# Half-size weight pieces, the extremes of the second weight taken inside the loop, and two row sums of each convolution's last half made from VectorE's moments

## The chip, the cores and the metric

The kernel runs on one core of a Trainium2 chip. Its engines are TensorE (PE, with its weight loads PEld), VectorE (DVE), ScalarE (ACT), GpSimd (POOL) and SyncE (SP), each with its own queue of instructions in a fixed order; transfers between HBM and SBUF run on 16 DMA engines and are issued here from SP and, a few, from ScalarE. The metric is the time of one execution on the device in microseconds: the median of three runs before the change is 2258.8 us (2254.0 to 2258.85).

## The reference

Two layers on an image batch x of shape (8, 256, 56, 56) in float32, each added to its input:

```python
x = x + involution(group_norm(x))      # layer 0
x = x + tri_block(group_norm(x))       # layer 1

def involution(x):                      # 7x7 kernels made per pixel, 16 groups
    ker = w_span @ (w_reduce @ x + b_reduce) + b_span
    out = (ker * patches_7x7(x)).sum(axis=3)

def tri_block(x):
    out1 = relu(batch_norm(noised_tri_conv(x, w1)))
    out2 = batch_norm(noised_tri_conv(out1, w2))
    return relu(out1 + out2)

def noised_tri_conv(x, w):              # 3x3, 256 to 256 channels
    tw = w - mean(w)
    mx, mn = max(tw), min(tw)
    lo, hi = mn + (mx - mn) / 3, mx - (mx - mn) / 3
    tq = where(tw < lo, -1, where(tw > hi, 1, 0))
    return conv(x, tq) + einsum(x, tq[:, :, 1, 1])
```

Two things matter for the change. A weight can be made ternary only when its mean, maximum and minimum over all its elements are known. And batch_norm needs the mean and variance of a convolution's whole output, over all eight images, before anything behind it can begin.

## The kernel before

The kernel has four stages, one after the other.

**The start** (L591 to L922). SP loads the first image (L545), then both weights whole into one buffer, `wf` (L631, four transfers), then 16 stores of zeros from the tile `xn` into the DRAM scratch `xtd` (L637). GpSimd may fill `xn` with data only when these stores have read it. `params(0)` finds group norm's factors of image 0. A loop over the three rows py of a tile then runs, for each, one strip of `prep` (GpSimd's `spread` into xn, a transpose on TensorE, ScalarE's copy into `stg`, a store to xtd), `reduce` (the pk matrix products, L651, copied into `kr` by ScalarE, L656), and three steps of `found`. `found` chains the searches for the extremes of both weights (`extremes`): for each sixth of a weight (768 elements in each partition) VectorE takes a maximum (L208) and a minimum (L209), and ScalarE a sum (L210, in place). When the sixths are done, two small steps on TensorE combine the partitions (`ends_w`, L222; `all_w`, L230), and some ten tiny VectorE instructions make mean, lo and hi in `cols`. After that `generate(0, 0, ...)` makes the first quarter's matrices: 14 units of pg matrix products (L782), each read out of PSUM into `a` by VectorE (L791) and ScalarE (L786). The pg products have two PSUM buffers. Further strips, the tile xe's parts (`surround`) and steps of `found` are put between the units.

**The loop** (L940 to L988) has 32 quarters of images with ten rows each, 320 rows. A row applies the matrices (pa, L815, on TensorE), picks the result out (L827 on ScalarE, L828 on VectorE, L831 on GpSimd), and, for the next quarter and the next image, does one or two units of `generate`, a strip, a part of xe, statistics (L150) and loads. `pin` keeps the order of the text on every engine. From row 8 on, every row also takes one step of `quant`, which makes the weights ternary and transforms them for the convolution: 16 pieces of each of the two weights, seven steps a piece, with one piece buffer (`piece_of`). A piece is fetched (L257), compared with hi and lo (L261, L262), subtracted (L264), combined into planes (L277 to L284) and stored (L287) by way of the list `tasks`, which `transfer` empties at the head of a row. In `params`, one step apart, TensorE makes `br` (L576) from the new factors and VectorE adds it into `brn` (L579).

**Two convolutions** (`conv_phase`) run over 16 half images each. For each, six groups of products (L464, in ORDER 1, 2, 3, 4, 0, 5) are combined into four interleaved rows y. Their sums and sums of squares are taken by ScalarE with an accumulating activation (`sums`, L416), one half image behind. In the last half image there is no half image left behind which to do that: `last_rows` takes rows 1 and 2 after group 4, row 0 after group 0, and row 3 after group 5, each of the latter two with four activations of 392 elements and a read of the accumulator for each. `batch_norm_params` (L177 and on) adds the columns of `stats` up; the columns are 2B + 2, since the last half image has three.

**The final stage** (L1052 to L1065) reads y1, y2 and x1 back tile by tile (16 tiles of 1.6 MB of each), combines them with two activations and two VectorE instructions, and stores the output. y1 and y2 have two buffers, x1 three. The first activation of a tile needs only the first convolution's factors; everything else needs the second's.

Of the kernel before, what the change touches and what calls it, by code (L numbers as in the profile page):

```python
# [80 lines left out]

QN, QJ = 96, 3 * C // 96
QS = WT
SLOT = (0, 2, 3, 4, 5, 1)
QM = 6


@with_exitstack
def involution_tri_block_kernel(
# [20 lines left out]
    def const_tile(shape, name):  # L110
        return const.tile(shape, F32, tag=name, name=name)
# [11 lines left out]

    st1, st2 = (const_tile([P, CT, 2, 2 * B + 2], name) for name in ("st1", "st2"))

# [66 lines left out]
    def piece_of(pool, name):  # L192
        return pool.tile([P, (4 + QS) * QN], F32, tag="piece", name=f"piece_{name}")

    def extremes(w, cols, pool, transposer, psum_tile, name):

# [6 lines left out]

        s, mx, mn = col(QM), col(QM), col(QM)
        f = nf // QM
        for j in range(QM):
            v = w[:, j * f:(j + 1) * f]
            nc.vector.tensor_reduce(mx[:, j:j + 1], v, AX.X, ALU.max)  # L208
            nc.vector.tensor_reduce(mn[:, j:j + 1], v, AX.X, ALU.min)  # L209
            nc.scalar.activation(v, v, AF.Identity, accum_out=s[:, j:j + 1])  # L210
            yield
        sums, ends = col(), col(2)
# [5 lines left out]
        nc.vector.memset(v[:, :P], 1.0)  # L218
        yield

        ps = psum_tile(f"ends_{name}")
        nc.tensor.matmul(ps[:, P:P + 1], v[:, :P], sums, start=True, stop=True)  # L222
        nc.tensor.transpose(ps[:2, :P], ends, transposer)
        mean, top = cols[:, 0:1], col()
        nc.vector.tensor_scalar(mean, ps[:, P:P + 1], 1.0 / (P * nf), None, ALU.mult)
        nc.vector.tensor_reduce(top[:2], ps[:2, :P], AX.X, ALU.max)
        nc.vector.tensor_copy(v[:2, P:2 * P], top[:2].to_broadcast([2, P]))
        yield
        ps = psum_tile(f"all_{name}")
        nc.tensor.transpose(ps[:, :2], v[:2, P:2 * P], transposer[:2, :2])  # L230
        ex = col(2)
        nc.vector.tensor_copy(ex, ps[:, :2])
# [4 lines left out]

        d, q0, r, th = (col() for _ in range(4))
        nc.vector.tensor_tensor(d, amx, amn, ALU.subtract)
# [7 lines left out]

    def quantize(dst, w_dram, cols, pool, tasks, name):


        mean, lo, hi = (cols[:, k:k + 1] for k in range(3))
        for t in range(CT):
            for j in range(QJ):
                v = piece_of(pool, name)
                w, u = v[:, :3 * QN], v[:, 3 * QN:]
                o = (t * QJ + j) * 3 * QN
                nc.sync.dma_start(w, w_dram[:, o:o + 3 * QN])  # L257
                yield
                yield
                g = u[:, :3 * QN]  # L260
                nc.vector.tensor_scalar(g, w, mean, hi, ALU.subtract, ALU.is_gt)  # L261
                nc.vector.tensor_scalar(w, w, mean, lo, ALU.subtract, ALU.is_lt)  # L262
                yield
                nc.vector.tensor_tensor(g, g, w, ALU.subtract)  # L264

                def part(x, k):
                    return x[:, k * QN:(k + 1) * QN]


                c0, c1 = max(C, j * QN) - j * QN, min(2 * C, (j + 1) * QN) - j * QN  # L270
                if c0 < c1:
                    g1 = part(u, 0)[:, c0:c1]
                    nc.vector.tensor_scalar(g1, g1, 2.0, None, ALU.mult)

                e, f = part(w, 0), part(w, 1)
                g1, g0, g2 = (part(u, k) for k in range(3))
                nc.vector.tensor_tensor(e, g0, g2, ALU.add)  # L277
                yield
                nc.vector.scalar_tensor_tensor(f, g2, 4.0, g0, ALU.mult, ALU.add)
                nc.vector.tensor_tensor(part(u, 3), e, g1, ALU.add)  # L280
                nc.vector.tensor_tensor(part(u, 4), e, g1, ALU.subtract)
                yield
                nc.vector.scalar_tensor_tensor(part(u, 5), g1, 2.0, f, ALU.mult, ALU.add)
                nc.vector.scalar_tensor_tensor(part(u, 6), g1, -2.0, f, ALU.mult, ALU.add)  # L284

                def store(u=u[:, QN:], o=t * 3 * C + j * QN):
                    nc.sync.dma_start(  # L287
                        bass.AP(dst[:].tensor, dst[:].offset + o,
                                [[QS * CT * 3 * C, P], [CT * 3 * C, QS], [1, QN]]), u)

                tasks.append(store)
                yield
                yield

# [20 lines left out]
    def conv_phase(i, begun, src_d, norm, stats, shift, dst_d, follow):  # L315
# [104 lines left out]
        def last_rows(n, y, k0, m):  # L420

            for _ in sums(n, [y[:, to].rearrange("p (r k) -> p r k", k=4 * W)
                              [:, :, k0 * W:(k0 + m) * W] for to in range(CT)]):
                pass

        done = iter(())
        nxt, begun = {}, ({}, None)
# [6 lines left out]
        for n in range(2 * B):  # L434
# [22 lines left out]
            for k in ORDER:  # L457
# [34 lines left out]
                elif k == 0:  # L492
                    row_of(0, m[0], 1.5, s, ALU.add)
                    if final:
                        last_rows(n + 1, y, 0, 1)
                elif k == 5:
                    row_of(3, m[5], 6.0, d, ALU.add)
                    if final:
                        last_rows(n + 2, y, 3, 1)
                next(steps, None)  # L500
# [17 lines left out]
    with ExitStack() as ph1:  # L518
# [6 lines left out]
        def ps_one(name):  # L525
            return ps_a.tile([P, 512], F32, tag="pt", name=name)
# [30 lines left out]
        def params(b):  # L557
# [13 lines left out]
            prm[b], prm_edge[b] = dst, edge  # L571
            yield
            ps = ps_one(f"br_{b}")
            for c in range(NCQ):
# [48 lines left out]
        for v in xe:  # L623
            nc.gpsimd.memset(v, 0.0)

        nf = CT * 9 * C
        wf = apool1.tile([P, A_COLS], F32, tag="a1", name="wf")
        for i, v in enumerate((w1, w2)):
            for j in range(2):
                o = j * nf // 2  # L630
                nc.sync.dma_start(wf[:, i * nf + o:i * nf + o + nf // 2], v[:, o:o + nf // 2])  # L631
        zero = xn.rearrange("p k r x -> p (k r x)")

        for d in (d for ds in xt_d for d in ds):
            for r0, n in ((0, PAD), (PAD + HH, HQ - PAD - HH)):
                e = n * QX * RP // P
                nc.sync.dma_start(  # L637
                    bass.AP(d[:].tensor, d[:].offset + r0 * QX * RP, [[e, P], [1, e]]), zero[:, :e])

        def reduce(b, py):  # L640
# [251 lines left out]
        for _ in params(0):  # L892
            pass
        strips, around = prep(0), surround(0, 0)
        a_next = matrices(0)
        thresholds = [pieces.tile([P, 32], F32, tag=f"cols{i}", name=f"cols{i}") for i in range(2)]
        ext = [extremes(wf[:, i * nf:(i + 1) * nf], thresholds[i], pieces, ident_sb, ps_one, f"w{i}")
               for i in range(2)]

        found = chain(*(islice(v, QM) for v in ext), *ext)  # L900

        for py in range(PY):
            next(strips)
            transfer(len(tasks))
            reduce(0, py)
            for _ in range(3):
                next(found)
# [25 lines left out]
        for k in rows[:QLEAD]:  # L933
            transpose_q(*k)
        pin()
        norm = iter(())
        quant = chain(*(quantize(wq_d[i], v, thresholds[i], pieces, tasks, f"w{i + 1}")
                        for i, v in enumerate((w1, w2))))
        last = None
# [197 lines left out]
```

## Time and profile before

| what | value |
|---|---|
| median of the runs | 2258.8 us |
| the profiled execution, whole | 2269.48 us |
| its span, first to last instruction | 2267.7 us |
| mean granted TensorE clock | 0.924 |
| PE busy | 1866.4 us, 82% |
| DVE busy | 1706.7 us, 75% |
| ACT busy | 1268.3 us, 56% |
| POOL busy | 584.5 us, 26% |
| HBM traffic | 264.05 MB read, 142.48 MB written |

In the trace the first row of the loop begins at 79.4 us, the last of its rows ends near 1149, the first convolution's products run from 1155.95 to 1584.7, the second's from 1600.7 to 2029, and the final stage from there to the end. A row of the loop takes some 3.4 us. The page's second part divides the span into 40 equal slices, with a digit for each engine's busy tenths; a window gives the same for any stretch, in microseconds, with the DMA rate; the timeline lists instructions in order of time with the idle time before each and what ended it. An average over the whole span mixes stages with different limits, so each stage is read by itself.

### The profile page before, as it was taken

To read this page: it belongs to the slowest core of one execution; us is meant where nothing else is said; L and a number is where in the kernel's file an instruction comes from. 1 tells how busy PE (TensorE), PEld (TensorE's weight loads), DVE (VectorE), ACT (ScalarE), POOL (GpSimd) and SP (SyncE) were. 2 spreads that over 40 slices of the span, in tenths; PEclk is the share of its full clock that TensorE was granted. 3 is DMA by queue.
4 is the path that set the end of the run, shared out by engine and by line. 5 is a ranking of instruction groups with operands and counts; after the bars stand their busy time and mean duration, and the time that the engine had idled before them with its cause. 6 is when DMAs were issued, how large, how long until landed. Compare 5 with 4: busy or idle time off the path is not lost.

```text
span 2267.7 us, 72706 instructions
## 1 busy us (share of the span) xinstructions
PE 1866.4 (82%) x31088; PEld 1716.6 (76%) x31088; DVE 1706.7 (75%) x2906; ACT 1268.3 (56%) x2461; POOL 584.5 (26%) x1320
## 2 busy tenths in 40 slices
PE   4889899898998989999879999999799999970000
PEld 3778777777877877778779999999799999970000
DVE  6676857667585775655689999998999999975444
ACT  3555455455554645556446766665576666673434
POOL 2545546364563645546400000000000000000000
PEclk9899999999999999999989999999899999995555
DMA  6556646566474754645453333334333333369999
GB/s 211 154 157 181 199 131 206 147 192 189 131 221 120 225 164 138 197 119 160 138 206 116 129 134 140 119 116 161 133 138 117 116 116 116 116 255 401 410 430 403
DMA packets 156447, 411.24 MB, mean 181 GB/s; under 512 B 51550, under 2 KB 62172, under 8 KB 148444
## 3 DMA queue, kind: packets, MB, share of 16 engines
q1 hardware_dynamic: 150528, 376.56, 49.9%
q10 hardware_dynamic: 5596, 30.03, 3.2%
q8 instruction: 245, 4.01, 0.8%
q14 instruction: 78, 0.64, 0.1%
HBM read 264.05 MB, written 142.48 MB: 179 GB/s over the span
## 4 chain that ended last, share of the span: by engine, by line
PE 38%; DMA 7%; DVE 3%; ACT 1%; issue 1%; ACTq 0%; SPq 0%; POOL 0%; DVEq 0%
PE c L464 37%; DMA y1f<-y1d 3%; DMA x1f<-x1d 2%; DMA out_y<-x1f 1%; DVE x1f L1064 1%; DMA y2f<-y2d 1%; ACT dummy L416 1%; DVE y1f L1062 0%; ACT y1f L1061 0%; ACT y1f L1063 0%; PE pa L815 0%; PE ptq L749 0%; DVE q L346 0%; DVE r L366 0%; DVE u L373 0%
## 5 line engine op out<-in xcount | busy, mean ns | idle before, releaser
L464 PE MATMUL c<-pl,wq 128*128 128x392 f32 x4608 | 857.1, 348 | 20.2 <-ACT pl L351 20.2
L464 PEld LDWEIGHTS c<-pl,wq 128*128 128x128 f32 x4608 | 855.1, 189 | 22.0 <-ACT pl L351 20.7
L791 DVE TENSOR_TENSOR a<-pg,bt 126x756 f32<-126x756 f32 (+3 forms) x640 | 393.2, 656 | 192.7 <-ACT a L786 147.3
L782 PE MATMUL pg<-kr,wl 64*126 64x140 f32 (+1 forms) x6144 | 459.4, 294 | 14.3 <-DVE a L791 7.1
L782 PEld LDWEIGHTS pg<-kr,wl 64*126 64x126 f32 x6144 | 396.8, 196 | 66.4 <-issue 41.5
L815 PE MATMUL pa<-a,q 126*32 126x48 f32 x17920 | 273.2, 208 | 62.3 <-issue 38.5
L815 PEld LDWEIGHTS pa<-a,q 126*32 126x32 f32 x17920 | 223.1, 111 | 115.8 <-issue 53.4
L786 ACT ACTIVATE a<-pg,bt 126x126 f32<-126x126 f32 x768 | 243.3, 475 | 102.6 <-PE pg L782 102.4
L831 POOL TENSOR_TENSOR x<-x,inv 128x168 f32<-128x168 f32 x320 | 166.4, 520 | 438.5 <-DVE inv L828 375.5
L828 DVE SCALAR_TENSOR_TENSOR inv<-pa,half_sb,inv 128x168 f32<-128x168 f32 x320 | 117.1, 366 | 171.0 <-ACT inv L827 144.8
L351 ACT CAST pl<-r 128x812 fp32r<-128x812 f32 x192 | 162.5, 868 | 145.2 <-DVE r L346 126.9
L752 ACT COPY q<-ptq 126x384 f32<-126x384 f32 x320 | 138.2, 481 | 162.7 <-issue 96.2
L331 POOL MEMSET xp<- 128x116 f32 x32 | 6.3, 195 | 829.4 <-DVE a L346 829.4
L416 ACT ACTIVATE dummy<-y,nc 128x1568 f32<-128x1568 f32 (+2 forms) x144 | 210.1, 1459 | 5.3 <-DVE y L484 3.5
L674 POOL TENSOR_SCALAR xn<-x,gn 128x224 f32<-128x224 f32 (+2 forms) x384 | 179.1, 486 | 130.0 <-PE pt L717 70.8
L352 DVE TENSOR_TENSOR pl<-r,pl 128x812 fp32r<-128x812 f32 x192 | 187.2, 1002 | 28.2 <-ACT pl L351 27.0
L674 POOL TENSOR_SCALAR xe<-x,gn 128x168 f32<-128x168 f32 (+2 forms) x384 | 161.2, 439 | 0.0
L720 ACT COPY stg<-pt 98x512 f32<-98x512 f32 x128 | 74.9, 585 | 137.0 <-issue 88.5
L749 PE MATMUL ptq<-ident_sb,xe 128*126 128x128 f32 x960 | 144.2, 285 | 4.6 <-DVE var_a L170 2.6
L150 DVE BATCH_NORM_STATS2 st<-x 128x6 f32<-128x392 f32 x256 | 138.3, 557 | 11.8 <-DMA x<-in_x 10.2
L827 ACT ACTIVATE inv<-pa,half_sb 128x168 f32<-128x168 f32 x320 | 128.2, 401 | 26.8 <-PE pa L815 25.7
L1011 ACT ACTIVATE xp<-raw,gn 128x392 f32<-128x392 f32 (+1 forms) x124 | 82.6, 721 | 62.9 <-DVE a L346 58.9
(144 smaller groups left out, 1846.2 us busy)
## 6 DMA issues: line engine op xcount, KB each, us to landing
q<-xtd SPq DMA_DIRECT2D x320, 252.0 KB
raw<-x1d SPq DMA_DIRECT2D x32, 812.0 KB
raw<-y1d SPq DMA_DIRECT2D x32, 812.0 KB
x<-in_x SPq DMA_DIRECT2D x64, 392.0 KB
xtd<-stg SPq DMA_DIRECT2D x128, 196.0 KB
x1d<-x SPq DMA_DIRECT2D x64, 392.0 KB
y1d<-y SPq DMA_DIRECT2D x30, 784.0 KB
y2d<-y SPq DMA_DIRECT2D x30, 784.0 KB
```

Of the source, the lines that this page charges most:

```text
L150: nc.vector.bn_stats(st[:, j, :], xt[:, j * NC:(j + 1) * NC])
L351: nc.scalar.copy(hi, r)
L352: nc.vector.tensor_tensor(lo, r, hi.bitcast(F32), ALU.subtract)
L416: nc.scalar.activation(dst, v, f, bias=shift[:, to:to + 1], accum_out=stats[:, to, j, n:n + 1])
L464: nc.tensor.matmul(ps[:, to, :NM], wq[k][:, t, dx, to * P:(to + 1) * P], part[:, t, :, dx:dx + W], start=(c == 0), stop=(c == last))
L674: nc.gpsimd.tensor_scalar(dst[:, i - d - k0:f - d - k0, :, x0:x0 + n], v[:, i:f, :, j0:j0 + n], scale, bias, ALU.mult, ALU.add)
L749: nc.tensor.transpose(pt[:NQ, k * P:(k + 1) * P], xe[c % 2][:, k, PY * ty:PY * ty + QY].rearrange("p r x -> p (r x)"), ident_sb)
L782: nc.tensor.matmul(dst, wl[rows, c, gp, o:o + NQ], kr[py][rows, px, :], start=True, stop=True)
L786: nc.scalar.activation(whole[:, g0 + i, p0 + j], ps[:NQ, i, j * nt:(j + 1) * nt], AF.Identity, bias=bt[:, c, g0 + i, p0 + j:p0 + j + 1])
L791: nc.vector.tensor_tensor(dst[:, g0:g0 + 2, p0:p0 + nv].rearrange("q g p t -> q g t p"), ps[:NQ, :, t0 * nv:t1 * nv].rearrange("q i (t p) ...
L815: nc.tensor.matmul(ps[o:o + 32, k * 2 * n:(k + 1) * 2 * n], q[:NQ, k, o:o + 32], av[:, t + k, g * 2 * n:(g + 1) * 2 * n], start=True, stop ...
L831: nc.gpsimd.tensor_tensor(xv, xv, iv.rearrange("p t (y x) -> p y t x", x=PX), ALU.add)
```

## The change

- The 16 stores of zeros are issued ahead of the weight; only w1 is loaded at the start and searched there as before, in six sixths, with two steps of `found` in each pass of the py loop instead of three.
- w2 is searched inside the loop, between the quantizing of w1 and that of w2. It is fetched in 12 pieces of 384 elements, and VectorE takes the sum as well as the extremes.
- Pieces are half as long (48 output channels instead of 96), there are 32 of each weight, and the piece tile has two buffers. `paced` runs fetch, `ternary`, `planes_of` and `store` of a piece at fixed rounds (0, 2, 3, 6), two pieces in seven rounds. A store is issued in its own round, not by way of `tasks`. The weights' layout in DRAM follows the new sizes.
- In the last half image of a convolution, rows 0 and 3 are no longer summed by ScalarE: VectorE takes their moments (`row_stats`) and, after row 3, turns the moments of both into sums (`row_sums`). `stats` has one column less.
- `params` has one more yield before the br products.

The order in which the final stage's instructions are issued moves too, though its text does not: before, tiles 3 and 4, and 5 and 6, run in pairs on ScalarE, VectorE and SP and the tiles from the seventh on one by one; now they run one by one from the third tile on, and the third x1 load is issued behind the third y2 and y1 loads instead of ahead of them.

```diff
-QN, QJ = 96, 3 * C // 96
+QN, QJ = 48, 3 * C // 48
-QM = 6
+QM, QM2 = 6, 12
...
-        return pool.tile([P, (4 + QS) * QN], F32, tag="piece", name=f"piece_{name}")
+        return pool.tile([P, (4 + QS) * QN], F32, tag="piece", bufs=2, name=f"piece_{name}")
+    def paced(events):
+        for r in range(max(events) + 1):
+            for f in events.get(r, ()):
+                f()
+            yield
...
+        def fetch(j):
+            held[j] = piece_of(pool, name)[:, :f]
+            nc.sync.dma_start(held[j], w_dram[:, j * f:(j + 1) * f])
+        def seek(j):
+            v = w[:, j * f:(j + 1) * f] if w is not None else held[j]
             nc.vector.tensor_reduce(mx[:, j:j + 1], v, AX.X, ALU.max)
             nc.vector.tensor_reduce(mn[:, j:j + 1], v, AX.X, ALU.min)
-            nc.scalar.activation(v, v, AF.Identity, accum_out=s[:, j:j + 1])
-            yield
+            if w is not None:
+                nc.scalar.activation(v, v, AF.Identity, accum_out=s[:, j:j + 1])
+        def add(j):
+            nc.vector.tensor_reduce(s[:, j:j + 1], held.pop(j), AX.X, ALU.add)
+        events = {}
+        for j in range(n):
+            if w is not None:
+                events[j] = [lambda j=j: seek(j)]
+            else:
+                r = 5 * (j // 2) + j % 2 * 2
+                events.setdefault(r, []).append(lambda j=j: fetch(j))
+                events.setdefault(r + 2, []).append(lambda j=j: seek(j))
+                events.setdefault(r + 3, []).append(lambda j=j: add(j))
+        yield from paced(events)
...
+        events = {}
+        for k in range(CT * QJ):
+            r = 7 * (k // 2) + k % 2 * 3
+            for n, f in ((0, fetch), (2, ternary), (3, planes_of), (6, store)):
+                events.setdefault(r + n, []).append(lambda f=f, k=k: f(k))
+        yield from paced(events)
...
+        def row_stats(st, y, k, j):
+            for to in range(CT):
+                v = y[:, to].rearrange("p (r k) -> p r k", k=4 * W)[:, :, k * W:(k + 1) * W]
+                nc.vector.bn_stats(st[:, to, j], v)
+        def row_sums(n, st):
+            mv = st[:, :, 2, :2]
+            for to in range(CT):
+                nc.vector.bn_aggr(mv[:, to, :], st[:, to, :2].rearrange("p n s -> p (n s)"))
+            sq = st[:, :, 2, 2]
+            nc.vector.tensor_tensor(mv[:, :, 0], mv[:, :, 0], shift, ALU.add)
+            nc.vector.tensor_tensor(sq, mv[:, :, 0], mv[:, :, 0], ALU.mult)
+            nc.vector.tensor_tensor(mv[:, :, 1], mv[:, :, 1], sq, ALU.add)
+            nc.vector.tensor_scalar(stats[:, :, :, n], mv, 2.0 * HT * W, None, ALU.mult)
...
                     if final:
-                        last_rows(n + 1, y, 0, 1)
+                        moments = half("s2").rearrange("p o r w -> p o (r w)")[
+                            :, :, :18].rearrange("p o (n s) -> p o n s", s=6)
+                        row_stats(moments, y, 0, 0)
...
                     if final:
-                        last_rows(n + 2, y, 3, 1)
+                        row_stats(moments, y, 3, 1)
+                        row_sums(n + 1, moments)
...
-        for i, v in enumerate((w1, w2)):
-            for j in range(2):
-                o = j * nf // 2
-                nc.sync.dma_start(wf[:, i * nf + o:i * nf + o + nf // 2], v[:, o:o + nf // 2])
...
+        for j in range(2):
+            o = j * nf // 2
+            nc.sync.dma_start(wf[:, o:o + nf // 2], w1[:, o:o + nf // 2])
...
-        found = chain(*(islice(v, QM) for v in ext), *ext)
+        found = ext[0]
...
-            for _ in range(3):
+            for _ in range(2):
                 next(found)
...
-        quant = chain(*(quantize(wq_d[i], v, thresholds[i], pieces, tasks, f"w{i + 1}")
-                        for i, v in enumerate((w1, w2))))
+        made = [quantize(wq_d[i], v, thresholds[i], pieces, f"w{i + 1}")
+                for i, v in enumerate((w1, w2))]
+        quant = chain(made[0], ext[1], made[1])
```

## The prediction

> **What bounds the kernel now.** I read four views in this order: the page's slices, to split the span; the timeline of the start; windows by image for the long loop; timeline and windows of the two convolution ends and of the final stage. In the slices, PE and DMA busy tenths:
>
> ```profile
>
> DMA  6556646566474754645453333334333333369999
> ```
>
> A slice is 56.7 us. Slices 3 to 35 are TensorE's: the loop (320 rows, from 79 us to 1149) and two convolutions (1156 to 1584, 1601 to 2029). The first slice is not, and in the last four DMA is full. A removed stall at the start, or at a convolution's end, shortens the time at once; work added to VectorE in the loop counts only as far as TensorE waits for it; in the final stage only DMA gaps count. The start, from the timeline:
>
> ```profile
> 35.59 1.34 POOL L674 TENSOR_SCALAR xn<-x,gn 128x224 f32<-128x224 f32 x3 [31.85 <-DMA xtd<-xn]
> 36.98 1.09 PE L717 MATMUL pt<-ident_sb,xn 128*98 128x128 f32 x4 [5.59 <-POOL xn L674]
> ...
> 47.27 0.98 PE L782 MATMUL pg<-kr,wl 64*126 64x140 f32 x12
> ...
> 79.37 0.27 PE L815 MATMUL pa<-a,q 126*32 126x48 f32 x2
> ```
>
> Columns: start, duration, engine, instruction, and in brackets the idle time before it and what ended it. GpSimd may not overwrite xn until its zeros are in DRAM (L637), which SP issued behind both weights (L631); TensorE waits 5.59 us for it. 47.27 is the first matrix product of the first quarter, 79.37 the first row of the loop.
>
> **Start: two edits, one answer.** The zeros go ahead of the weight, and w2's 2.36 MB are not loaded here. DMA ran full from 10 to 30 us (349 to 424 GB/s in windows of 5 us). Images, constants and zeros are about 6.2 MB; by 25 us 7.7 MB had moved. So the zeros land near 25 us, not 35.5, and w1 (2.36 MB, 6 us at 400 GB/s) by about 30. VectorE's six pairs of reductions (12 x 0.86 us, start to start) then end near 37 to 39, ScalarE's sums following. TensorE ends its first pk group at 31.4 as before, transposes at once, and runs the two other groups (4.95 and 3.67 us) to about 40.5: first pg near 41, **6 us earlier**. ScalarE executes w1's sums in the same queue, ahead of the kr copies; should the weight land 4 us later, 4 of the 6 us are lost.
> From first pg to first pa took 32.1 us. Strips paced the first five units at 2.2 us; later TensorE idled 3.3 us before ends_w at 59.8 and 1.5 us before w2's at 67.7, and its clock fell to 0.52 to 0.79 in four windows of 5 us from 55 to 75. In the changed order six ScalarE sums of 1.03 us, five pairs of reductions (9 us of VectorE) and w2's ends_w and all_w leave this stretch. The strips' pace and ScalarE's 24 activations of a remain. Without the two stalls (4.8 us), and with a little less time at low clock, I estimate 26 us: another 6 us. **Start: -12 us, from -5 to -15.**
>
> **Loop: what is added.** Views by image (windows between every 40th L828):
>
> ```profile
> 353.00:491.00 138.00, 123.03 (x3314) 104.82 (x3312) 96.67 (x237) 73.74 (x201) 72.62 (x160) 0.99 0.58 169
> 629.00:766.00 137.00, 124.30 (x3316) 106.05 (x3314) 94.89 (x229) 73.41 (x202) 71.88 (x160) 0.98 0.62 174
> 905.00:1040.00 135.00, 124.15 (x3308) 106.37 (x3307) 81.95 (x179) 72.77 (x201) 69.95 (x160) 0.96 0.55 157
> ```
>
> Columns: window, length, busy us (count) of PE, PEld, DVE, ACT, POOL, clock, DMA share, GB/s. The third image has no quantizing (32 pieces x 7 rows from row 8 end at row 232). It has 13.8 us less VectorE than the mean of the two others and is about 2.5 us shorter: 0.18 us of time for 1 us of VectorE. VectorE's rows:
>
> ```profile
> L264 DVE TENSOR_TENSOR piece_w<-piece_w 128x288 f32<-128x288 f32 x32 | 15.8, 494 | 0.0
> L280 DVE TENSOR_TENSOR piece_w<-piece_w 128x96 f32<-128x96 f32 x32 | 8.8, 274 | 0.0
> ```
>
> Undisturbed they are 0.45 and 0.25 us, so about 0.15 us plus 1 ns an element. A piece is 3 of the first kind, 6 of the second and sometimes one of L273: 2.9 us. A half piece is 3 x 0.30 + 6 x 0.20 + 0.1 = 2.2; a pair 4.4: +1.5 us x 32 = 48 us. w2's extremes: 12 x 3 reductions of 384 elements, 0.55 each by the same line (the 768-element row took 0.95): 20 us. Together 68 us of VectorE, x 0.18 = **+12 us**.
> [...] But in the timeline independent 96-element instructions start 0.16 to 0.17 us apart though each lasts 0.25, so about 0.07 to 0.1 us of the fixed part is covered by the neighbour: 304 x 0.1 = 30 us, with w2's 17 us 47 us of occupied VectorE, x 0.18 = 8.5 us. Bounds: +3 (a fit over rows by quantizing phase gives a third of a us per 7 rows, 0.11 a us of VectorE, of 30 us) and +20 (0.3 a us). I take **+8**: the second sum, since the timeline shows the overlap.
> Hidden at no cost: SP's 64 fetches and 64 stores instead of 32 and 32, and w2's 12 fetches; SP waited over 410 us for pa in the loop, and the stores, now three rows behind their data, no longer hold it (104 us at L287). DMA share is 0.6: the 384-byte store packets took 24 ns each; 49,152 of 192 bytes at some 15 ns are 11 us more over 16 engines in 900 us. If that cover were gone, q loads would be late, and TensorE shows no such wait now. [...] Quantizing now ends at row 275, 45 rows before the loop does. The extra yield in params leaves br's matmuls at the same place on TensorE (seven waits of 1.6 us stay) and puts brn on VectorE behind two additions: nothing.
>
> **Convolution ends.**
>
> ```profile
> 1584.75 1.04 DVE L450 SCALAR_TENSOR_TENSOR y<-c,d 128x392 f32<-128x392 f32 x2 [1.44 <-PE c L464]
> ...
> 1590.29 0.23 DVE L177 TENSOR_REDUCE bmv_bn<-st 128x4 f32<-128x72 f32 x1 [4.50 <-ACT dummy L416]
> ...
> 2037.35 0.23 DVE L177 TENSOR_REDUCE bmv_bn<-st 128x4 f32<-128x72 f32 x1 [7.25 <-ACT dummy L416]
> ```
>
> L177 waits for ScalarE's row sums (0.75 us each, eight of 392 elements). They go. VectorE gets two bn_stats after row 0 (in its gap before row 3) and after row 3: 2 x 0.5, two aggregations (0.27, smaller here: 0.2), four tiny dependent steps (0.2 start to start): 2.3 us after 1585.75, so 1588.1. ScalarE's remaining sums end at 1584.3. Next late is VectorE itself. **-2.2 us**, and TensorE's second convolution starts so much earlier. At the second end row 3 is written at 2030.0, the sums are ready at 2032.3 (ScalarE's last at 2031.4): 5 us sooner. But DMA is full there:
>
> ```profile
> 2080.00:2090.00 10.00, 0.00 (x0) 0.00 (x0) 3.22 (x1) 0.00 (x0) 0.00 (x0) 0.50 0.92 341
> ...
> 2100.00:2110.00 10.00, 0.00 (x0) 0.00 (x0) 8.14 (x3) 6.39 (x3) 0.00 (x0) 0.50 0.96 375
> 2110.00:2120.00 10.00, 0.00 (x0) 0.00 (x0) 2.02 (x1) 0.69 (x1) 0.00 (x0) 0.50 0.91 385
> ...
> 2150.00:2160.00 10.00, 0.00 (x0) 0.00 (x0) 6.06 (x2) 2.91 (x1) 0.00 (x0) 0.50 1.00 428
> ```
>
> What counts is bytes not moved. Against 430 GB/s these three windows lack 1.9 MB, 4.4 us, and 2044 to 2056 lacks 0.7 MB, 1.7 us. The dips lie where the instructions run in pairs of images; the changed order leaves the pairing after the first pair, as the old order did from 2130 on at 428 GB/s. But one x1 load less is issued ahead of the wait at 2038, so a first dip stays. **-4 us, from -1 to -6.**
>
> **Sum:** -12 + 8 - 2 - 4 = -10 us: from the profiled execution's 2269.5 (span 2267.7) to 2259.5. The runs' median, 2258.8, lies 10.7 below the profiled one; the same -10 there gives **2249**.
>
> **Rivals.** (a) Forecast, 2244 to 2252: 0.48. (b) VectorE's work hides almost wholly (VectorE idles 300 us in the loop waiting for ScalarE): loop +3, others as said, -15: below 2244, centre 2242 with the start's upper bound: 0.22. For it: fit by rows; against it: the shorter third image. (c) The loop takes back nearly all: start only -8, loop +12, ends -4, the lower bounds but for the loop: no change, about 2259: 0.22. For it: ScalarE's sums of w1 stand ahead of the kr copies, and the clock may fall in the shorter start as well; against it: DMA was full there, so w1's landing follows from bytes alone. (d) Slower: longer VectorE blocks (1.2 us behind a row's additions, where 0.85 was the longest) push the additions that free pg's two PSUM buffers, TensorE waits at L782/L815. It decides from 0.37 us per us of VectorE (68 x 0.37 = 25 us against 18 gained, the rest being what a measurement can tell; at 0.45 the time is 2271): 0.08. For it: 23 existing pa waits for DVE a; against: those are 18.8 us in all.
> About 0.3%, 6.8 us, is what a measurement can tell from no change. So faster 0.70, same 0.23, slower 0.07. Range 2237 to 2263: it leaves out part of (d) and the end of (b).
>
> **What would show it.** First xn on POOL near 25 us, first pg near 41, first pa near 67; images 139 to 140 us up to row 275; L177 near 2.3 us after the last L450; final stage without windows under 400 GB/s after the first 20 us. The forecast is wrong if w1's late landing stalls the kr copies, if images are over 143 us, or if the final stage keeps its length.

## The result and the profile after

The changed kernel takes 2251.4 us (median of 20 runs, 2242.9 to 2261.4) where the kernel before takes 2258.6 beside it (20 runs, 2248.4 to 2269.8): ratio 0.9964, 95% interval 0.9951 to 0.9977, that is -8 us with -5 to -11. Beside later experiments the same kernel came to 0.9929 (0.9907 to 0.9951). In the three sets of the experiments the kernel before has medians of 2263.8, 2263.2 and 2262.1 us, and 2262.4 over all its 125 runs; the changed kernel's 26 runs have 2251.3. Over all sets the change is so worth -11 us (-10 to -13, by drawing the runs again at random). Medians of one kernel in different sets can differ by 5 us, and kernels that ran in different sets are to be compared with that in mind. The profiled execution of after took 2249.66 us (span 2247.9), 1.8 below its median; that of before stood 10.9 above the median of these 20 runs. So the 19.8 us between the two traces are not the effect, and each stage has to be read with that in mind.

The slices of the page of after, busy tenths of TensorE and of the DMA engines:

```profile
PE   5989898898989889889889999999899999980000
DMA  6647658475475755755453333334333333369999
```

TensorE's row in the page of before:

```profile
PE   4889899898998989999879999999799999970000
```

The structure is the old one: the first slice has a tenth more of TensorE, and no other stretch changes its character. By stage, from the starts of the first and last instruction of each in the two traces (us):

| stage | before | after | difference | predicted |
|---|---|---|---|---|
| start to first pg | 47.3 | 39.2 | -8.0 | -6 |
| first pg to first pa | 32.1 | 22.3 | -9.8 | -6 |
| loop, first pa to last picked row, as traced | 1068.0 | 1070.9 | +2.9 | |
| loop, set to the median | 1057.2 | 1072.6 | +15.4 | +8 |
| last product to first of the next convolution | 16.35 | 13.94 | -2.4 | -2.2 |
| the two convolutions together | 856.4 | 857.4 | +1 | 0 |
| last product to the end | 239.0 | 235.6 | -3.4 | -4 |

"Set to the median" takes from the loop what the profiled execution lies above the median of its kernel's runs. Three kernels of this study have the loop of before unaltered: before, e1_ends_only and e2_zeros_first. Their traced loops are 1068.0, 1057.7 and 1079.6 us, and their profiled executions lie 10.9, 0.1 and 20.3 us above their medians. The difference comes to 1057.2, 1057.6 and 1059.3. So the scatter of 20 us is in the loop, and the loop of before at the median is 1058; by the median of all 125 runs it is 1061. The loop's loss is 12 to 15 us.

**The start.** Timeline of after (start, duration, engine, instruction, idle time before it and what ended it):

```profile
25.78 1.34 POOL L734 TENSOR_SCALAR xn<-x,gn 128x224 f32<-128x224 f32 x3 [22.03 <-DVE brn L640]
29.35 0.95 DVE L223 TENSOR_REDUCE cols<-wf 128x1 f32<-128x768 f32 x1 [3.93 <-DMA wf<-in_w]
39.26 0.88 PE L842 MATMUL pg<-kr,wl 64*126 64x140 f32 x12
61.54 0.27 PE L875 MATMUL pa<-a,q 126*32 126x48 f32 x2
```

GpSimd no longer waits for its zeros: what releases it is the image's own brn. The weight is in at 29.3. Three windows of before in the stretch between first pg and first pa (window, length, busy us and count of PE, PEld, DVE, ACT, POOL, then granted clock, DMA share, GB/s):

```profile
57.00:62.00 5.00, 2.17 (x17) 1.95 (x18) 2.53 (x10) 2.50 (x9) 2.43 (x6) 0.57 0.43 120
62.00:67.00 5.00, 4.23 (x39) 3.46 (x37) 2.81 (x12) 2.44 (x7) 1.51 (x4) 0.75 0.57 184
67.00:72.00 5.00, 4.26 (x27) 3.46 (x28) 3.83 (x18) 0.00 (x0) 3.28 (x9) 0.59 0.09 30
```

and two of after in the same stretch:

```profile
49.00:54.00 5.00, 4.02 (x56) 3.32 (x52) 3.40 (x5) 2.69 (x8) 4.16 (x11) 1.00 0.89 275
54.00:59.00 5.00, 3.71 (x52) 3.02 (x50) 3.00 (x8) 2.34 (x7) 5.00 (x13) 1.00 0.37 104
```

Read the clock and the counts in parentheses together: TensorE is about as busy as in the second and third window of before, but with 52 to 56 matrix products in 5 us where it had 17 to 39. The two waits for ends_w are gone, and so is the low clock around them.

**The ends.** VectorE's timeline of after at the end of the first convolution, and the same step of the second:

```profile
1569.75 1.04 DVE L507 SCALAR_TENSOR_TENSOR y<-c,d 128x392 f32<-128x392 f32 x2 [0.49 <-PE c L521]
1570.70 1.03 DVE L470 BATCH_NORM_STATS2 s<-y 128x6 f32<-128x392 f32 x2
1571.64 0.33 DVE L476 BATCH_NORM_AGGREGATE s<-s 128x2 f32<-128x12 f32 x2
...
1572.88 0.22 DVE L177 TENSOR_REDUCE bmv_bn<-st 128x4 f32<-128x68 f32 x1
...
2015.80 0.22 DVE L177 TENSOR_REDUCE bmv_bn<-st 128x4 f32<-128x68 f32 x1
```

No idle time stands before L177: it follows 3.1 us after the start of the last row, where it was 5.5. Windows of the final stage of after:

```profile
2025.00:2030.00 5.00, 0.00 (x0) 0.00 (x0) 5.00 (x3) 2.91 (x1) 0.00 (x0) 0.50 0.86 316
...
2080.00:2090.00 10.00, 0.00 (x0) 0.00 (x0) 3.52 (x2) 5.40 (x2) 0.00 (x0) 0.50 1.00 428
2100.00:2110.00 10.00, 0.00 (x0) 0.00 (x0) 5.91 (x2) 2.91 (x1) 0.00 (x0) 0.50 1.00 424
2110.00:2120.00 10.00, 0.00 (x0) 0.00 (x0) 3.84 (x2) 4.67 (x2) 0.00 (x0) 0.50 1.02 435
```

The early dip stays, the later three are gone.

### The profile page after: what moved, and what is told of

Its sections match the earlier page's. It is cut to its first block, busy times and chain, and to the rows that moved or that the text cites. A ratio compares the mean times of both kernels' runs of the same rounds, so it can differ in the third digit from the quotient of the medians.

```text
span 2247.9 us, 73156 instructions
## 1 busy us (share of the span) xinstructions
PE 1849.4 (82%) x31088; PEld 1701.1 (76%) x31088; DVE 1757.2 (78%) x3246; ACT 1252.6 (56%) x2417; POOL 580.1 (26%) x1320
## 5 line engine op out<-in xcount | busy, mean ns | idle before, releaser
L521 PE MATMUL c<-pl,wq 128*128 128x392 f32 x4608 | 858.1, 349 | 17.8 <-ACT pl L391 17.8
L521 PEld LDWEIGHTS c<-pl,wq 128*128 128x128 f32 x4608 | 856.1, 190 | 19.6 <-ACT pl L391 18.3
L842 PE MATMUL pg<-kr,wl 64*126 64x140 f32 (+1 forms) x6144 | 447.6, 288 | 24.5 <-DVE a L851 14.2
L842 PEld LDWEIGHTS pg<-kr,wl 64*126 64x126 f32 x6144 | 385.2, 190 | 75.7 <-issue 42.8
L392 DVE TENSOR_TENSOR pl<-r,pl 128x812 fp32r<-128x812 f32 x192 | 187.1, 1001 | 29.3 <-ACT pl L391 28.1
L456 ACT ACTIVATE dummy<-y,nc 128x1568 f32<-128x1568 f32 (+1 forms) x128 | 200.1, 1563 | 4.8 <-DVE y L541 3.5
```

Source lines behind the costliest of these rows:

```text
L392: nc.vector.tensor_tensor(lo, r, hi.bitcast(F32), ALU.subtract)
L456: nc.scalar.activation(dst, v, f, bias=shift[:, to:to + 1], accum_out=stats[:, to, j, n:n + 1])
L521: nc.tensor.matmul(ps[:, to, :NM], wq[k][:, t, dx, to * P:(to + 1) * P], part[:, t, :, dx:dx + W], start=(c == 0), stop=(c == last))
L842: nc.tensor.matmul(dst, wl[rows, c, gp, o:o + NQ], kr[py][rows, px, :], start=True, stop=True)
```

## Experiments

The theory after the result: the start gave 18 us and the ends 6, and the loop took 12 to 15 of them back. The rivals: the loop is nearly untouched, and the gains of start and ends are smaller than one trace says; or a price that is not VectorE's, of SyncE's waits or of short packets, is what the loop pays. In the excerpts of code "..." stands for lines left out. All times are medians; ratios are to the kernel before on the same chip.

**1. The ends alone.** In before, with the two helpers and the narrower `stats` of the change:

```diff
-last_rows(n + 1, y, 0, 1)
...
+row_stats(moments, y, 0, 0)
...
-last_rows(n + 2, y, 3, 1)
+row_stats(moments, y, 3, 1)
+row_sums(n + 1, moments)
```

> The kernel before, with only the two row sums of the last half image moved to VectorE's moments. Theory A (both ends gain as the two traces show, -2.4 us between the convolutions and -3.4 us in the final stage): -6 us, 0.9974 of before; the statistics step L177 comes about 2.5 us after the last product of each convolution. Rival B (the final stage is bound by bytes, so its shorter length belongs to another order of its instructions or to chance, not to this edit): -2.4 us, 0.9989, and the stretch from the last product to the end stays at 239 us.

Measured: 0.9957 (0.9941 to 0.9973). The gap between the convolutions is 13.93 us, the last product stands 235.3 us before the end, as in the changed kernel. Theory A: 2.4 and 3.7 us. The final stage's gain comes with this edit, not with the rest of the change; whether by the earlier factors or by the other order of its instructions was not told apart. The ratio's middle, -10 us, is more than the trace's stages show; -6 is at the edge of its interval.

**2. The zeros first, alone.** In before, the block that loads wf, both weights, moves behind the stores of zeros:

```diff
-for i, v in enumerate((w1, w2)):
-    for j in range(2):
-        o = j * nf // 2
-        nc.sync.dma_start(wf[:, i * nf + o:i * nf + o + nf // 2], v[:, o:o + nf // 2])
 zero = xn.rearrange("p k r x -> p (k r x)")
 for d in (d for ds in xt_d for d in ds):
...
+for i, v in enumerate((w1, w2)):
+    for j in range(2):
+        o = j * nf // 2
+        nc.sync.dma_start(wf[:, i * nf + o:i * nf + o + nf // 2], v[:, o:o + nf // 2])
```

> The kernel before, with only the order of the start's transfers changed: zeros ahead of both weights, both weights still loaded and searched there. Theory A (the wait for xn was one of two causes): GpSimd's first xn at 25 us, first pg near 41, first pa near 72, -6 us or 0.9973 of before; the rest of the start's gain belongs to w2's search leaving it. Rival B (the start has slack behind the wait: the later landing of the weights takes the gain back at the extremes): first pa within 2 us of before's 79, ratio 1.000. Rival C (the order of the zeros is the whole gain of the start): first pa near 62, -16 us, 0.993.

Measured: 0.9983 (0.9961 to 1.0005); first pg 42.1, first pa 76.1. From TensorE's timeline of this kernel:

```profile
42.15 0.98 PE L783 MATMUL pg<-kr,wl 64*126 64x140 f32 x12 [1.49 <-ACT kr L657]
...
56.59 0.56 PE L222 MATMUL ends_w<-cols,piece_w 128*128 128x1 f32 x2 [2.38 <-DVE piece_w L218]
...
64.49 0.44 PE L222 MATMUL ends_w<-cols,piece_w 128*128 128x1 f32 x2 [1.51 <-DVE piece_w L218]
...
76.14 0.27 PE L816 MATMUL pa<-a,q 126*32 126x48 f32 x2
```

Five of the 6 us arrive at first pg, two go again behind it, where both waits for ends_w still stand (2.38 and 1.51 us; 3.3 and 1.5 before). Theory A in kind, with 3.2 us where it had 6 to 7. Rival C falls: the zeros are some fifth of the start's gain.

**3. Whole pieces in the changed kernel.**

```diff
-QN, QJ = 48, 3 * C // 48
-QM, QM2 = 6, 12
+QN, QJ = 96, 3 * C // 96
+QM, QM2 = 6, 6
...
-tag="piece", bufs=2,
+tag="piece",
...
-r = 5 * (j // 2) + j % 2 * 2
+r = 5 * j
...
-r = 7 * (k // 2) + k % 2 * 3
+r = 7 * k
...
```

> The changed kernel with pieces of 96 output channels in one buffer again (16 pieces of each weight, one per seven rounds, w2 searched in 6 pieces of 768): about 48 us less busy VectorE in the loop, fewer and longer store packets. Theory A (0.18 us of time for 1 us of occupied VectorE, 30 to 48 us): 5 to 9 us shorter than the changed kernel, 0.9925 to 0.994 of before. Rival B (VectorE's added work is hidden): as the changed kernel, 0.9964 within 0.001. Rival D (0.37 or more): 11 to 18 us shorter, 0.988 to 0.991.

Measured: 0.9916 (0.9884 to 0.9948), 2243.8 us; loop at the median 1064. Repeated in a later set:

> The kernel of e3_full_pieces once more, beside these: 0.9916 of before within 0.002; loop 1064 us at the median, 7 to 8 us less than the changed kernel's 1071 to 1072.

Measured: 0.9895 (0.9860 to 0.9929), 2239.1 us, loop 1061. That is 7.5 and 12.3 us below the changed kernel's 26 runs, which come from other sets; the first ratio's interval overlaps with that of experiment 5, the second lies a little beyond what was expected of it. By the loops, half pieces cost 7 to 11 us; rival B falls. Theory A's size fits, but not yet its cause.

**4. More of VectorE's work.** In the changed kernel:

```diff
-(3, planes_of), (6, store)
+(3, planes_of), (3, planes_of), (6, store)
```

> The changed kernel with the five plane instructions of each half piece executed twice: 320 instructions of 48 elements (the second set writes the same values), 64 us more busy VectorE, some 53 us by the distance of starts. Theory A (0.18 us of time for 1 us): +9 us against the changed kernel, 1.0004 of before, spread over the images up to row 275. Rival B (hidden): +0 to +3 us, 0.996 to 0.9977. Rival D (0.37 or more): +20 us or more, 1.005.

Measured: 1.0018 (1.0003 to 1.0032), 15 us more than the changed kernel (2266.5 against 2251.3 for its 26 runs in two sets), loop 1087. The window of the whole loop has 812 us of busy VectorE against 769: 43 us, so 0.35 us of time for 1 us, between theory A and rival D. Where it goes, in the groups of TensorE: before, the changed kernel, then this one (busy us and mean ns, then idle time before the group and its releasers):

```profile
L782 PE MATMUL pg<-kr,wl 64*126 64x140 f32 (+1 forms) x6144 | 459.4, 294 | 14.3 <-DVE a L791 7.1 <-issue 6.1 <-DVE piece_w L279 0.3
```

```profile
L842 PE MATMUL pg<-kr,wl 64*126 64x140 f32 (+1 forms) x6144 | 447.6, 288 | 24.5 <-DVE a L851 14.2 <-issue 5.2 <-DVE piece_w L315 4.6
```

```profile
L842 PE MATMUL pg<-kr,wl 64*126 64x140 f32 (+1 forms) x6144 | 453.8, 291 | 36.0 <-DVE a L851 25.6 <-DVE piece_w L315 5.4 <-issue 4.1
```

The wait for the additions of a, which free pg's PSUM buffers, has grown by 11 us. This is the mechanism of the prediction's rival (d), at about the price of its threshold, with a block of planes that is 0.68 us of busy VectorE longer (43.3 us over 64 half pieces). In a smaller measure it is at work in the changed kernel itself: against before, pg waits 7 us longer for the additions and 4 for the planes.

**5. The changed kernel again**, as the partner of the next three.

> The changed kernel itself, beside the three others of this set. By the runs so far: 0.9964 of before. Reading of the loop (first pa to the last row of the loop, set against the distance of the profiled execution from the median): theory A says 1072 +- 3 us at the median, where before has 1057 to 1059 by three profiles, so the loop takes back +15 us; rival B (loop hidden) says that a second profile lands at 1060.

Measured: 0.9929 (0.9907 to 0.9951), 2249.9 us. The profiled execution is 9.1 us below this median, its loop 1062.1, so 1071 at the median: theory A. Without that correction the trace alone would have said rival B.

**6. No search of w2.**

```diff
-quant = chain(made[0], ext[1], made[1])
+quant = chain(*made)
...
-quantize(wq_d[i], v, thresholds[i], pieces, f"w{i + 1}")
+quantize(wq_d[i], v, thresholds[0], pieces, f"w{i + 1}")
```

> The changed kernel without the search of w2: the 12 fetches, the 36 reductions and the small steps behind them are left out, and w2 is made ternary with the mean and the bounds of w1. Theory A (VectorE's 20 us of reductions at 0.2 to 0.3 us per us, plus two small TensorE steps): -4 to -7 us against the changed kernel, 0.9935 to 0.9945 of before. Rival B (hidden): 0.9964 within 0.001. Quantizing ends 30 rows earlier, no other step moves.

Measured: 0.9914 (0.9893 to 0.9935), 2244.5 us, 5.4 below the changed kernel beside it, loop 1066. Theory A; with six runs of each the size is good to some 5 us, and rival B is only made unlikely by it.

**7. w2 searched at the start again**, and loaded there behind w1.

```diff
...
-extremes(None, w2, thresholds[1], pieces, ident_sb, ps_one, "w1")]
-found = ext[0]
+extremes(wf[:, nf:2 * nf], w2, thresholds[1], pieces, ident_sb, ps_one, "w1")]
+found = chain(*(islice(v, QM) for v in ext), *ext)
...
-for _ in range(2):
+for _ in range(3):
     next(found)
...
-quant = chain(made[0], ext[1], made[1])
+quant = chain(*made)
```

> The changed kernel with w2 loaded and searched at the start again, behind w1 (three steps of found in each pass), half pieces and the ends as changed. Theory A (w2's leaving gave some 14 of the start's 18 us, its search costs 4 to 7 us in the loop): first pa near 75 us, +8 us against the changed kernel, 1.000 of before. Rival C (the start's gain is the zeros', and the search in the loop is dear): first pa near 65, 0.994 of before.

Measured: 0.9987 (0.9972 to 1.0001), 2260.1 us; first pg 42.1, first pa 74.7, loop at the median 1068. Theory A: w2's leaving is worth 13.4 us of the start, 3.2 at first pg and 10.3 behind it, and costs 3 to 5 us in the loop.

**8. Stores twice, to the same place and to another.**

```diff
-(6, store)
+(6, store_twice)
...
+def store_twice(k):
+    store(k)
+    store(k)
...
```

> The changed kernel with each of the 64 stores of half pieces issued twice (the same bytes): 49,152 more packets of 192 bytes in the loop, no more VectorE work. Theory A (the small packets are hidden, the half pieces cost by VectorE): 0.9964 of before within 0.0015, loop as the changed kernel's. Rival E (half pieces cost the loop by their short packets, by q loads that come late): +5 to +9 us, 0.999 to 1.0005.

Measured: 1.0420 (1.0394 to 1.0446), 2358.6 us, 108 more than the changed kernel beside it. Neither theory had that. SyncE's queue waits in this kernel (line that waits, releaser, total, times, longest):

```profile
SPq L323 <- DMA wqd<-piece_w: 272.0, 64, 8.1
```

and the group of VectorE that reads the fetched half pieces:

```profile
L299 DVE TENSOR_SCALAR piece_w<-piece_w,cols 128x144 f32<-128x144 f32 x64 | 23.3, 364 | 86.9 <-DMA piece_w<-in_w 75.3 <-issue 7.0 <-DMA xtd<-stg 4.6
```

The second store of a pair writes where the first wrote, so it waits for the first to land, 64 times 4.25 us, and it waits in SyncE's queue: what stands behind it there is issued late. VectorE then stands 75 us for fetched pieces, where the changed kernel has no such time, and TensorE 54 us for q loads. The test had added a wait, not only packets. So it was done again with a place of its own for the second store:

```diff
+aside = dram.tile([P, QS * CT * 3 * C], F32, tag="aside", name="aside")
...
+def store_aside(k):
+    store(k, aside)
+    store(k)
...
-(6, store)
+(6, store_aside)
```

> The changed kernel with each of the 64 stores of half pieces issued a second time, into a DRAM tile of its own that nothing reads, so that the second waits for no landing of the first: 49,152 more packets of 192 bytes, no more VectorE work. Theory A (packets hidden): 0 to +3 us against the changed kernel. Rival E (the number of packets costs): +8 us or more, and TensorE's idle time for q at the row's products shows it. If it stays near the changed kernel, the +108 us of the run that stored twice to one place belong to SyncE's wait for the first store's landing (64 of 4.25 us).

Measured: 1.0022 (1.0007 to 1.0038), 2267.0 us, 16 more than the changed kernel; loop 1088. Rival E in size: the doubled traffic is not free. By subtraction the other 92 of the 108 us were the wait. Where the 16 arise the trace doesn't show: TensorE's wait for q is under 1 us, contrary to the expectation; its busy time in the loop is 969 us against 956 and the granted clock 0.97 against 0.98, but two traces of one and the same loop differ as much (965 and 953, see the last section). Packets, their 9.4 MB and 64 more issues on SyncE were not told apart.

**9. The fetch one row later.** The waits of experiment 8 pointed to a small sister in the changed kernel. SyncE's waits for stores to land in before, then in the changed kernel:

```profile
SPq L257 <- DMA wqd<-piece_w: 31.1, 20, 3.4
```

```profile
SPq L294 <- DMA wqd<-piece_w: 103.9, 50, 4.5
```

A half piece goes into the buffer that the last but one left, and that one's store was issued one row earlier (rounds 6 and 7); 50 of the 64 fetches wait some 2 us for it to land. In the changed kernel, and in the one of whole pieces:

```diff
-(0, fetch), (2, ternary), (3, planes_of), (6, store)
+(1, fetch), (3, ternary), (4, planes_of), (6, store)
```

> The changed kernel with each half piece fetched one row later, compared one row later and its planes one row later (rounds 1, 3, 4, store still 6): two rows instead of one lie between a store and the fetch that reuses its buffer. SyncE's 104 to 112 us of waits in L294 for the landing of the stores (some 50 of 2.2 us) should mostly go. Theory A (the half pieces cost by VectorE): as the changed kernel, within 2 us, loop 1070 to 1073 at the median. Rival F (they cost because SyncE, held by these waits, issues the rows' q loads late): -6 to -9 us, as much as whole pieces bring, 0.990 to 0.993 of before.

> Whole pieces in one buffer (as in e3_full_pieces), with the fetch, the comparison and the planes one row later. Theory A: as e3_full_pieces, 0.9916 of before within 0.002. Rival F (SyncE's waits for the store's landing, 40 us in e3_full_pieces, cost time): 2 to 4 us less than e3_full_pieces.

Measured with half pieces: 0.9912 (0.9878 to 0.9945), 2243.2 us, loop 1064; 8 us below the changed kernel's 26 runs (3 to 11 by resampling the runs of both; those 26 come from two other sets, and the ratio's interval overlaps with that of experiment 5). The wait is gone:

```profile
SPq L294 <- DMA wqd<-piece_w: 5.4, 5, 2.2
```

With whole pieces: 0.9903 (0.9871 to 0.9935), 2242.1 us, no better than without (2239.1 and 2243.8). So rival F has the size right for half pieces and not for whole ones, where 24 to 26 such waits (40 and 51 us in all) cost nothing that shows. And with the fetch later, half pieces (771 us of busy VectorE in the loop) and whole pieces (728) are 1.2 us apart (-3 to +6.5), in one set: 43 us more of VectorE, spread over the rows, are mostly hidden. The edit moves the comparisons and the planes by a row as well; that the wait and not this shift gives the 8 us is argued, not shown.

TensorE's waits for VectorE in the loop, added up in each trace, are 51 to 52 us in the three kernels with the loop of before, 68 and 74 in the two executions of the changed kernel, 62 to 66 in the three of whole pieces, 61 without the search of w2, 69 with half pieces fetched a row later, and 84 with the planes twice. So VectorE's added work is seen as time that TensorE waits for it, 16 to 22 us more than before in the changed kernel, and the later fetch leaves these waits as they are. Its 8 us are in no idle time that the traces tell apart: in experiment 5's execution SyncE waits 111.7 us for the same landings, and its loop took 1062.1 us, no longer than the 1062.7 with the later fetch. TensorE's waits without a releaser in the profile range from 25 to 59 us over these traces, too unevenly to settle 8 us. So the way from SyncE's waits to TensorE's time stays open, and with it whether they are the cause.

The best kernel of the study is whole pieces with all else as changed: 0.9895 and 0.9916 in its two sets, some 10 us less than the change as made (7 to 12 by resampling).

## Why the prediction was right, and where its steps were not

It gave 2249 with -10 us; measured were -8 (-5 to -11) in the set with the prediction's runs and -11 over all sets. That the middle came so near is luck: two errors cancel. The start gained 6 us more than predicted (-17.8, outside the start's own range of -5 to -15), the loop lost 4 to 7 more.

- *Start, zeros and weight.* First xn 25.8 (predicted near 25), weight at 29.3 (by about 30), first pg 39.2 (near 41). Right. Experiments 2 and 7 divide it otherwise than the text did: the zeros give 5 us at first pg, and w2's leaving 3 more, of which 2.1 to 2.3 are seen: in both of those kernels pg waits 1.49 us, and the last pk group 0.6 to 0.8, for ScalarE's kr copies, behind ScalarE's sums.
- *Start, first pg to first pa: mis-sized, 26 us predicted, 22.3 measured.* The term "a little less time at low clock" was mis-sized: with 4.8 us for the two stalls it is left 1.3 us. Before had 0.57 to 0.75 granted in the four windows from 57 to 77 us, the changed kernel 1.00 in all five, and TensorE's busy time in the stretch fell from 24.3 to 18.3 us for nearly the same products (231 and 228 instructions). In e1_ends_only, whose start is that of before, it was 22.0 in a stretch of 30.6, so the term is 4 to 6 us.
- *Loop: mis-sized, +8 predicted, +12 to +15 measured (1071 to 1073 against 1057 to 1061).* The mechanism, work on VectorE that TensorE has to wait for, is the one seen: these waits grew by 16 to 22 us with 57 us more of busy VectorE (769 against 712). One term of the sum was wrong, and perhaps a second. The first is the slope "0.18 us of time for 1 us of VectorE", taken from one image in one execution. It was 2.5 us of difference between images; in e1_ends_only and e2_zeros_first, with the same loop, the same three images give 3.8 and 6.9 us for the same 13.9 us of VectorE: 0.27 and 0.50. By images the loss can't be read either: the changed kernel's take 134 to 142 us in two traces (forecast 139 to 140), those of the three kernels with the loop of before 130 to 145. There is no one slope: spread work costs little (experiment 9), the same amount packed behind the planes costs 0.35 (experiment 4), the search of w2 3 to 7 us for 19 us of VectorE. The second, as far as is known, is "Hidden at no cost: SP's 64 fetches and 64 stores". The text counted SyncE's slack and the stores' own waits, but not that with two buffers each fetch comes one row behind the store of its buffer. With that fetch a row later the kernel is 8 us faster, in a comparison across sets; that SyncE's wait is what cost them is not shown.
- *The fixed part of VectorE's instructions: there, and mostly hidden.* The prediction worked out 0.15 us and 1 ns an element from two durations of before. The changed kernel agrees: its L301 (128x144) takes 334 ns in the mean where L264 (128x288) took 494, and its L316 (128x48) 210 where L280 (128x96) took 274. Half the elements so take 0.68 and 0.77 of the time. (The 304 of the prediction's sum are its count of the instructions that half pieces add; by the lines of the two traces there are 296.) The loop's busy time did grow: 43 us from whole to half pieces with the fetch later, of which 1 us (at most some 7) is seen in the time. The durations went into VectorE's busy time; in this loop the schedule around them decided the cost.
- *Small packets at nothing.* Not refuted for the change: the stores of half pieces carry 24,576 packets more than those of whole ones, and with the fetch later the two are 1.2 us apart. (The text's 11 us over the 16 engines are 9 by its own figures, 49,152 packets of 15 ns less 24,576 of 24. The traces have 15.3 ns in the mean for the 192-byte packets of the changed kernel and 24.1 for the 384-byte ones of before: 10 us.) But another 49,152 packets, with as many bytes again, cost 16 us, so the cover that the text named has an end; how much of this is packets, bytes or issues stays open.
- *Convolution end* -2.2 predicted, -2.4 measured, by the steps named: VectorE is next late. *Final stage* -4, measured -3.4 to -3.7: the three dips go, the first stays.
- *Rivals.* (b) had a loop of +3 and a start of up to -15, (c) a loop of +12 and a start of -8. The loop went as in (c) or a little beyond, the start beyond (b). (d) didn't decide, but its wait is there: 7 us more of it in the changed kernel, 11 more again in experiment 4.

## What to carry to other kernels

Before a slope is read from two stretches of one execution, compare the same stretches in a second execution of the same code: here identical loops differed by 20 us, more than all that was to be explained. When a buffer is made smaller and doubled, count the distance from the store of a buffer to the fetch that reuses it, in rows, and compare it with the store's time to land; in experiment 8 such waits for a landing, 4.25 us each in the mean, delayed what stood behind them in SyncE's queue and cost 92 us; with whole pieces 24 to 26 of them (40 and 51 us in all) cost nothing that shows. A stall of TensorE is to be priced with the low clock that follows, which at the start here was worth about as much as the stall (4 to 6 us against 4.8).

## What the runs showed of the hardware

**In the traces of before and after the low clock follows a sparse stretch.** In both, the record of the granted clock changes only at multiples of 3.41 us from one change to another: ahead of the final stage its stretches at half clock last 3.41, 6.83, 10.24 or 17.07 us. Windows of the changed kernel's loop, laid on these slices:

```profile
544.41:547.82 3.41, 1.59 (x60) 1.05 (x47) 3.00 (x11) 0.80 (x3) 0.54 (x1) 1.00 0.93 265
547.82:551.23 3.41, 2.59 (x30) 2.61 (x32) 3.15 (x15) 0.46 (x2) 0.01 (x1) 0.50 0.35 119
551.23:554.64 3.41, 3.41 (x78) 3.07 (x76) 1.12 (x2) 2.00 (x6) 3.07 (x7) 0.50 0.02 5
```

and TensorE's timeline there:

```profile
546.46 0.55 PE L809 MATMUL ptq<-ident_sb,xe 128*126 128x128 f32 x3 [1.00 <-DVE var_a L170]
548.64 1.01 PE L637 MATMUL br<-gn,wr 64*64 64x1 f32 x16 [1.64 <-DVE gn L173]
```

Waits of 1.00 and 1.64 us with little between them leave TensorE busy for 1.59 us of a slice, and the next 6.8 us run at half clock; behind a slice that is full it is 1.00 again. Of the loop's 302 slices at full clock, the ten behind which it fell had TensorE busy for 1.1 to 2.0 us, the 292 others for 1.9 or more. In before, 16 falls stand behind 1.1 to 2.0 us, and of the 277 slices that kept it one was busy for 1.6, the others for 1.9 or more. Five of the ten falls follow this same wait of 1.64 us at an image's br products. The longest single gap of TensorE in this loop's trace is 2.22 us, so no slice was idle throughout: the clock fell behind slices in which TensorE was busy for a third to three fifths of the time.

**The scatter between executions is not of one kind.** TensorE's busy time for the products of one and the same loop is 965 us in before, 953 in e1_ends_only and 965 in e2_zeros_first, at granted clocks of 0.97, 0.98 and 0.97 (16, 10 and 18 falls), with loops of 1068, 1058 and 1080. So the 10 us between the first two are low clock; the third has 11 us more idle TensorE than the first besides. The two executions of the changed kernel differ otherwise: with 956 and 958 us busy, at 0.98 both, their loops are 1070.9 and 1062.1, and TensorE is idle for 115 and 104. The wait that differs most stands between products of pa and has no releaser in the profile (us in total, times, longest; first execution, then that of experiment 5):

```profile
PE pa L875 <- issue: 38.2, 44, 2.1
```

```profile
PE pa L875 <- issue: 18.3, 23, 2.2
```

What ends it stays open.

**In experiment 8 the waits in SyncE's queue cost more than the second stores: 92 us against 16.** 64 waits of 4.25 us in SyncE's queue made the kernel some 92 us longer, by the difference of the two kernels of experiment 8. The loop of the changed kernel, then of the one that stores twice to one place (columns as above):

```profile
61.50:1132.40 1070.90, 955.82 (x26128) 816.11 (x26126) 769.11 (x2040) 572.89 (x1566) 550.91 (x1235) 0.98 0.61 171
```

```profile
61.60:1247.30 1185.70, 1006.74 (x26127) 860.88 (x26126) 769.07 (x2041) 575.66 (x1566) 552.38 (x1235) 0.93 0.60 162
```

Of 115 us more, 64 are idle TensorE, 54 of them for q loads, and 51 are the same products at a lower clock. SyncE issues these transfers and its queue shows the 64 waits (272.0 us in all); the q loads behind them came late, and so did the fetched pieces, for which VectorE stood 75 us.
